# The second layer's root product and the output product of a graph network, in seven block products instead of whole ones

## The chip, the cores and the metric

The kernel runs on one core of a Trainium2 chip, as one launch. The metric is the device time of that launch in microseconds (us), lower is better; the times below are medians of several runs. A profile is one execution taken by the hardware profiler. Its span goes from the first to the last instruction, and the device time of the same execution is a little longer.

## The reference, cut to what matters

Two graph blocks follow each other on 384 nodes with 1024 features, each with a layer norm ahead of it and a residual around it. The first is an attention block over a mask of edges. The second is a relational graph convolution of two layers on 768 features. All is in float32.

```python
x = relu(h_text @ w_in + b_in)
for l in range(2):
    h_in = x
    # per relation r: mean over the edges of type r, of x @ W[r], W = comp x basis
    x = _rgcn_conv(x, src, dst, edge_type, basis[l], comp[l], root[l], conv_bias[l])
    #   = agg + x @ root[l] + conv_bias[l]
    x = relu(x) + h_in
    x = _batchnorm(x, bn_gamma[l], bn_beta[l])   # over the nodes
h_final = x @ w_out + b_out                       # 384 x 768 times 768 x 1024
out = x_before + _layernorm(h_final, ln_gamma, ln_beta)
```

Two products are touched: `x @ root[l]` of the second layer (384 x 768 times 768 x 768) and `x @ w_out`.

## The kernel before, in words

The queues of TensorE (PE), VectorE (DVE), GpSimd (POOL) and SyncE (SP) follow the order in which the code is written, and from line 496 on ScalarE (ACT) does too. So the place of a call in the code is its place in its engine's queue. Tiles come from pools, with the waits between engines put in by the framework: who overwrites a buffer waits for all its readers. PSUM has eight banks, dealt in turn by `next_bank`. Weights go through `wload`, which takes one of five buffers in turn; SP issues those loads in order, so a load whose buffer isn't free holds up the ones behind it.

Features lie on partitions in the convolution (`XT`, `XN`: six chunks of 128 features by 384 nodes). Many products in this kernel are already done by halves: the three operands are cut in two each way, and seven products of quarter size stand in for eight, with sums and differences of the quarters made by DVE beforehand and the partial results gathered behind. In code this is `multiply` (L399) for the attention part and the input layer (L402 in the profile), and the local `times` in the convolution (L979 for the products by basis, L1077 for the aggregation over nodes). The products that are not cut are one plain accumulation over the six chunks.

The second block runs so:

- The input layer (L857 to L903) writes `XT`. DVE and ACT gather its quarters (L882, L883).
- For each layer and each of four basis matrices b, `XT` times the basis (L985 and L979) gives `H_`. `weight_sums` and `last_sums` (L927 to L935) make the differences of the weights, `node_sums` (L920) those of the nodes. `go_between` puts other work between the products: in the second layer it is `mix`, by which the adjacency tables `A` of the six relations are weighted into `At` (L346 and L348).
- The root product (L1014 to L1023) accumulates all six output chunks in six banks, 36 matmuls of 384 columns (L1019). `rest()`, the last product of the basis before it, comes in behind the first six.
- The aggregation (L1080 to L1162) works on three pairs of output chunks. It first makes the differences of `At` (L1082 to L1086) and the first `feature_sums` (L1097). A product of each pair is added to the root's banks; `begin` (L1063) then moves the banks to `XN` on ACT, with the convolution's bias. All later products are added to `XN` by DVE in `take` (L1107). PE writes a bank again only when `take` has read it. When a chunk is complete, ACT applies the ReLU (`rectify`, L1110), DVE adds the residual and takes statistics (`measure`, L1042 to L1049), and `normalise_layer` (L1054 to L1058) ends the chunk.
- In the second layer the rows `b_out`, `ln_gamma` and `ln_beta` are loaded by ACT's queue into the room of `A` (L1038).
- The output (L1169 to L1198) goes by blocks of 128 nodes, t = 0, 1, 2. POOL first adds `ln_beta` to the residual `x_sb` (L1170). Per block, PE does six matmuls for each part of the 1024 columns (L1183); DVE adds `b_out` and takes statistics (L1187, L1189), ACT takes a square root (L159), and DVE makes the norm and the residual in two steps for each half (L1194, L1197). Each half is stored at once, one by SP, one by ACT.

Of the kernel before, what the change touches and what calls it, by code (L numbers as in the profile page):

```python
# [10 lines left out]
F32 = mybir.dt.float32  # L11
# [3 lines left out]
AF = mybir.ActivationFunctionType  # L15
ALU = mybir.AluOpType

P = 128
# [10 lines left out]
HC = DC // 2  # L29
HN = N // 2  # L30
# [21 lines left out]
def gnn_kernel(ctx: ExitStack, tc: tile.TileContext, out, x, edges, chunks, cols, rows, small,  # L52
               wq, wk, wv, wiq, wik, wiv, wo, w_in, basis, root, w_out):
# [299 lines left out]
    def add_up(r):  # L353
        sums[r] = late.tile([P, N], F32, tag="sum", name="sum", bufs=4)
        nc.gpsimd.tensor_tensor(sums[r], A[:, r, 0, :], A[:, r, 1, :], ALU.add)
        nc.gpsimd.tensor_tensor(sums[r], sums[r], A[:, r, 2, :], ALU.add)

    def share(r):

        ps = next_bank("ps_cnt", [i for i in range(8) if i not in taken])  # L360
        nc.tensor.matmul(ps[:, :N], ones, sums[r], start=True, stop=True)
        rn = late.tile([P, N], F32, tag="rn", name="rn", bufs=2)

        nc.scalar.activation(rn, ps[:, :N], AF.Relu, bias=minus)
        nc.scalar.activation(rn, rn, AF.Identity, bias=ones[:, 0:1])
        nc.vector.reciprocal(rn, rn)
        nc.vector.tensor_tensor(A[:, r], A[:, r], rn[:, None, :].to_broadcast([P, NT, N]), ALU.mult)
        if r + 4 < R:
            add_up(r + 4)


    with ExitStack() as inner:
# [263 lines left out]
        A = late.tile([P, R, NT, N], F32, tag="A", name="A")  # L636

# [93 lines left out]
        for g in range(STEPS + 1):  # L731
            f = g + LEAD
            if g < STEPS:
                turn_probs(g)
            if f < STEPS:
                exponents(f)
            if f - 1 in total:
                normalise(f - 1)
            if f + 1 < STEPS:
                scores(f + 1)  # L740
            if g == STEPS:
                ps_y = next_bank("ps_y", (0,))
                multiply_o(ps_y, 2, 0, range(KD - 1))
            if g > 0:
                gather(g - 1)
            if f + 2 == STEPS:

                w_x = [act_tile("w_x") for _ in range(2)]
                for half in range(2):
                    load_rows(w_x[half], w_in[half])  # L750
                w_first = [wload(basis[0, 0, part], (2, DC), "w_c") for part in range(3)]
                w_first += [wload(basis[0, 1, part], (2, DC), "w_c") for part in range(2)]
        soft_stack.close()
# [118 lines left out]
        for p in range(3):  # L872
# [13 lines left out]
            add_up_quad(quads[0][0], pb)  # L886
            multiply(pc, s[:, 0], T[1], True)
# [18 lines left out]
    with tc.tile_pool(name="conv", bufs=1) as cp:  # L906
# [7 lines left out]

        def node_sums(X):
            S = cp.tile([P, 4, 3, P], F32, tag="S", name="S")
            for i, a, b, op in ((0, block(X, 1, 0), block(X, 1, 1), ALU.add), (1, S[:, 0], block(X, 0, 0), ALU.subtract),
                                (2, block(X, 0, 0), block(X, 1, 0), ALU.subtract),
                                (3, block(X, 0, 1), S[:, 1], ALU.subtract)):
                nc.vector.tensor_tensor(S[:, i], a, b, op)  # L920
            return S

        def weight_sums(w):
            T13 = keep.tile([P, 3, 2, HC], F32, tag="hT", name="T13")
            T2 = keep.tile([P, 3, HC], F32, tag="mask8", name="T2")
            for c in range(3):
                nc.vector.tensor_tensor(T13[:, c], w[c][:, :, HC:], w[c][:, 0, :].rearrange("p (o d) -> p o d", o=2),  # L927
                                        ALU.subtract)
                nc.vector.tensor_tensor(T2[:, c], w[c][:, 1, HC:], T13[:, c, 0], ALU.subtract)
            return T13[:, :, 0], T2, T13[:, :, 1]  # L930

        def last_sums(w, T2):
            T4 = cp.tile([P, 3, HC], F32, tag="T4", name="T4")
            for c in range(3):
                nc.vector.tensor_tensor(T4[:, c], w[c][:, 1, :HC], T2[:, c], ALU.subtract)  # L935
            return T4
# [19 lines left out]
        for i in range(10):  # L956
            between[1, (i + 1) // 3, (i + 1) % 3] = mixes(1, 1 + i // 2, *((0, 1), (2, 3))[i % 2])

# [6 lines left out]
        for l in range(L):  # L965
# [3 lines left out]
            for b in range(B):  # L969
# [23 lines left out]
                times(pc, S[:, 0], lambda c: T[0][:, c], True)  # L993
# [3 lines left out]
                times(pa, S[:, 1], lambda c: T[1][:, c])  # L997
                nc.scalar.copy(hs[0][1], pa)
                times(pc, S[:, 3], lambda c: w[c][:, 1, HC:])
                nc.vector.tensor_tensor(hs[0][1], hs[0][1], pc, ALU.add)  # L1000
                times(pa, S[:, 2], lambda c: T[2][:, c])
# [12 lines left out]
            w = [wload(root[l, part], (2, DC), "w_c") for part in range(3)]  # L1014
            XN = xtp.tile([P, KC, N], F32, tag="XT", name="XN")
            pr = [next_bank("ps_c", [i for i in range(8) if i not in kept])[:, :N] for _ in range(KC)]
            for k in range(KC):
# [6 lines left out]
            room2 = keep.tile([P, KD * N], F32, tag="hT", name="room2")  # L1024
            spaces = [room2[:, 2304:]]
            if l + 1 < L:
                spaces += [v.rearrange("p i k o -> p (i k o)")[:, i * 768:(i + 1) * 768] for v, n in
                           ((cp.tile([P, 4, 3, P], F32, tag="S", name="sums"), 2),
                            (wpool.tile([P, 2, 6, P], F32, tag="w", name="sums"), 2)) for i in range(n)]
                spaces.append(cp.tile([P, 3, HC], F32, tag="T4", name="sums").rearrange("p c d -> p (c d)")[:, :768])  # L1030
                w = load_basis(l + 1, 0)
            else:

                room = late.tile([P, R * NT * N], F32, tag="A", name="room")
                spaces += [room[:, 3 * D + i * 768:3 * D + (i + 1) * 768] for i in range(5)]
                rowsB = room[:, :3 * D].rearrange("p (j d) -> p j d", j=3)
                for j, r in enumerate((R_BOUT, R_LNG, R_LNB)):
                    nc.scalar.dma_start(rowsB[:, j, :], rows[r:r + 1, :].to_broadcast([P, D]))  # L1038

# [31 lines left out]
            def q(i, j):  # L1071

                return At.rearrange("p b n d -> p (b n) d")[:, i * 6:i * 6 + 6, j * HN:(j + 1) * HN]

# [5 lines left out]
            T1, T2 = [room2[:, i * 1152:(i + 1) * 1152].rearrange("p (c d) -> p c d", c=6) for i in range(2)]  # L1080
            T4 = keep.tile([P, 6, HN], F32, tag="mask8", name="T4")
            nc.vector.tensor_tensor(T1, q(0, 1), q(0, 0), ALU.subtract)  # L1082
            nc.vector.tensor_tensor(T2, q(1, 1), T1, ALU.subtract)
            T3 = q(0, 1)
            nc.vector.tensor_tensor(T3, q(1, 1), q(0, 1), ALU.subtract)
            nc.vector.tensor_tensor(T4, q(1, 0), T2, ALU.subtract)  # L1086
# [32 lines left out]
            for p in range(pairs):  # L1119
                times(pr[2 * p][:, :HN], h(2 * p, 1), q(1, 0))  # L1120
            for o in range(KC):
                begin(o)
            take(0, 0, pa)
            ready = None
            for p in range(pairs):
# [11 lines left out]
                next(sums, None)  # L1137
                times(pc, S[p][3], q(1, 1))
# [23 lines left out]
                pa = following  # L1162
            XT = XN
# [5 lines left out]
        for t in range(NT):  # L1169
            nc.gpsimd.tensor_tensor(x_sb[:, t, :], x_sb[:, t, :], rowsB[:, 2, :], ALU.add)  # L1170
        w = [wload(w_out[part], (2, D), "w_out") for part in range(3)]
        hf_ = cp.tile([P, NT, D], F32, tag="H", name="hf")
        for t in range(NT):
            hf = hf_[:, t, :]
            last = t == NT - 1
            ps = [next_bank("ps_f") for _ in range(3 if last else 2)]

            parts = [(ps[0], 0, 512), (ps[1][:, :256], 512, 768), (ps[2][:, :256], 768, D)] if last else \
                [(ps[0], 0, 512), (ps[1], 512, D)]
            for ks in ((range(4), range(4, KC)) if t == 0 else (range(KC),)):  # L1180
                for p, c0, c1 in parts:
                    for k in ks:
                        nc.tensor.matmul(p, XT[:, k, t * P:(t + 1) * P], w[k // 2][:, k % 2, c0:c1],  # L1183
                                         start=(k == 0), stop=(k == KC - 1))
            st = tiny.tile([P, 4, 6], F32, tag="st", name="st")
            for p, c0, c1 in parts:
                nc.vector.tensor_tensor(hf[:, c0:c1], p, rowsB[:, 0, c0:c1], ALU.add)  # L1187
                for c in range(c0, c1, 256):
                    nc.vector.bn_stats(st[:, c // 256, :], hf[:, c:c + 256])  # L1189
            mv, sd = row_spread(st)  # L1190

            parts = ((nc.sync, slice(0, 512)), (nc.scalar, slice(512, D)))
            for _, cs in parts:
                nc.vector.scalar_tensor_tensor(hf[:, cs], hf[:, cs], mv[:, 0:1], rowsB[:, 1, cs], ALU.subtract, ALU.mult)  # L1194
            nc.vector.reciprocal(sd, sd)
            for queue, cs in parts:
                nc.vector.scalar_tensor_tensor(hf[:, cs], hf[:, cs], sd, x_sb[:, t, cs], ALU.mult, ALU.add)  # L1197
                queue.dma_start(out[t * P:(t + 1) * P, cs], hf[:, cs])  # L1198

# [70 lines left out]
```

## Time and profile before

| | us |
|---|---|
| device time, median of 3 runs (715.83 to 717.43) | 715.99 |
| the profiled execution: device time | 717.47 |
| the profiled execution: span | 715.7 |
| PE busy in the span | 699.9 |
| DVE busy in the span | 512.6 |
| ACT busy in the span | 157.6 |
| POOL busy in the span | 308.1 |
| second layer's root product, chain (L1019) | 611.18 to 636.34, with 1.94 of L979 in it |
| second layer's aggregation, chain (L1077) | 636.34 to 677.29 |
| output product, chain (L1183) | 677.29 to 708.23 |

How to read the views. The page gives each engine's busy time, and the span in 40 slices with the busy share of each in tenths; `PEclk` is the clock that TensorE was granted. A f32 matmul shows as two records, so 36 matmuls are x72. The chain of waits is followed back from the last instruction to whatever released each one, and printed in order of time: start, length, engine, what, line. The timeline gives the instructions of an engine: start, busy time, engine, line, operation, output and inputs, count; in brackets the idle time before it and what ended it. Matmuls overlap in the pipeline, so that a group's busy time is a little longer than its step.

### The profile page before, as it was taken

To read this page: it belongs to the slowest core of one execution; us is meant where nothing else is said; L and a number is where in the kernel's file an instruction comes from. 1 tells how busy PE (TensorE), PEld (TensorE's weight loads), DVE (VectorE), ACT (ScalarE), POOL (GpSimd) and SP (SyncE) were. 2 spreads that over 40 slices of the span, in tenths; PEclk is the share of its full clock that TensorE was granted. 3 is DMA by queue.
4 is the path that set the end of the run, shared out by engine and by line. 5 is a ranking of instruction groups with operands and counts; after the bars stand their busy time and mean duration, and the time that the engine had idled before them with its cause. 6 is when DMAs were issued, how large, how long until landed. Compare 5 with 4: busy or idle time off the path is not lost.

```text
span 715.7 us, 9149 instructions
## 1 busy us (share of the span) xinstructions
PE 699.9 (98%) x3228; PEld 527.9 (74%) x3228; DVE 512.6 (72%) x1307; ACT 157.6 (22%) x360; POOL 308.1 (43%) x239
## 2 busy tenths in 40 slices
PE   8999999999999999999999999999999999999995
PEld 7759999999997444478985555558975555579943
DVE  5886697868886699787534279798878766507756
ACT  3211111111111577410221124202131111011100
POOL 1366777778687788687786542000000000120000
PEclk9999999999999999999999999999999999999999
DMA  8788787373562622733424994311104322700001
GB/s 303 267 279 264 228 250 212 80 243 67 203 209 43 177 2 1 221 44 45 89 0 103 250 288 153 133 44 45 45 0 133 102 69 94 308 1 1 1 30 59
DMA packets 69180, 91.04 MB, mean 127 GB/s; under 512 B 22940, under 2 KB 50688, under 8 KB 68750
## 3 DMA queue, kind: packets, MB, share of 16 engines
q1 hardware_dynamic: 46830, 78.45, 32.6%
q0 software_dynamic: 21296, 9.60, 10.8%
q10 hardware_dynamic: 1008, 2.41, 0.9%
q8 instruction: 25, 0.41, 0.2%
q14 instruction: 21, 0.17, 0.1%
HBM read 79.27 MB, written 11.16 MB: 126 GB/s over the span
## 4 chain that ended last, share of the span: by engine, by line
PE 87%; DVE 10%; ACT 2%; DMA 1%; issue 0%; DVEq 0%; ACTq 0%
PE ps_g L985 12%; PE ps_g L979 10%; PE ps_k L402 10%; PE ps_c L1077 10%; PE ps_v L402 8%; PE ps_q L420 6%; PE ps_q L402 5%; PE ps_f L1183 4%; DVE At L348 4%; PE ps_y L402 3%; PE ps_c L1019 3%; PE ps_x L402 3%; PE ps_o L707 2%; PE ps_s L662 2%; PE ps_pT L696 2%; PE ps_v L586 2%
## 5 line engine op out<-in xcount | busy, mean ns | idle before, releaser
L283 POOL DMA_INDIRECT atab<-count,at x99 | 166.3, 1679 | 44.2 <-issue 23.5
L278 POOL DMA_INDIRECT mtab<-m_val,at x99 | 103.4, 1045 | 57.6 <-issue 22.9
L1170 POOL TENSOR_TENSOR x_sb<-x_sb,room 128x1024 f32<-128x1024 f32 x3 | 7.0, 2348 | 188.9 <-DMA room<-in_rows 188.9
L348 DVE SCALAR_TENSOR_TENSOR At<-A,small_sb,At 128x1152 f32<-128x1152 f32 x40 | 53.6, 1414 | 0.0
L979 PE MATMUL ps_g<-T,S 128*128 128x384 f32 x144 | 49.1, 486 | 0.0
L985 PE MATMUL ps_g<-w_c,XN 128*128 128x384 f32 x144 | 47.7, 487 | 1.1 <-DVE XN L1107 1.1
L985 PE MATMUL ps_g<-w_c,XT 128*128 128x384 f32 x144 | 47.9, 486 | 0.0
L420 PE MATMUL ps_q<-hT,w_q 128*128 128x384 f32 (+1 forms) x160 | 43.4, 435 | 1.4 <-DVE hT L108 1.4
L985 PEld LDWEIGHTS ps_g<-w_c,XN 128*128 128x128 f32 x144 | 27.3, 190 | 20.2 <-DVE XN L1107 1.4
L979 PEld LDWEIGHTS ps_g<-T,S 128*128 128x128 f32 x144 | 27.3, 190 | 19.2 <-ACT H L991 0.4
L985 PEld LDWEIGHTS ps_g<-w_c,XT 128*128 128x128 f32 x144 | 27.3, 190 | 18.8
L420 PEld LDWEIGHTS ps_q<-hT,w_q 128*128 128x128 f32 x160 | 30.1, 200 | 14.1 <-ACT hT L101 1.7
L1077 PE MATMUL ps_c<-At,H 128*128 128x192 f32 x216 | 36.4, 326 | 0.0
L1077 PEld LDWEIGHTS ps_c<-At,H 128*128 128x128 f32 x216 | 35.4, 190 | 0.5
L402 PE MATMUL ps_k<-T,S 128*128 128x192 f32 x192 | 35.1, 326 | 0.0
L1107 DVE TENSOR_TENSOR XN<-XN,ps_c 128x192 f32<-128x192 f32 x38 | 12.5, 349 | 30.8 <-ACT XN L1063 19.7
L402 PEld LDWEIGHTS ps_k<-T,S 128*128 128x128 f32 x192 | 31.8, 190 | 0.0
L1183 PE MATMUL ps_f<-w_out,XN 128*128 128x512 f32 (+1 forms) x84 | 31.1, 531 | 0.0
L675 DVE CUSTOM_DVE_ANT_0 s<-ps_s,mask 128x384 f32<-128x384 f32 x48 | 24.5, 550 | 5.3 <-PE ps_s L662 5.3
L267 DVE SCALAR_TENSOR_TENSOR same<-cells,own,later 128x128 f32<-128x128 int32 x99 | 28.0, 350 | 0.4
L267 DVE SCALAR_TENSOR_TENSOR same<-keys,key,weigh 128x128 f32<-128x128 int32 x99 | 27.9, 349 | 0.0
L1183 PEld LDWEIGHTS ps_f<-w_out,XN 128*128 128x128 f32 x84 | 15.9, 190 | 14.9 <-issue 14.3
(298 smaller groups left out, 1411.6 us busy)
## 6 DMA issues: line engine op xcount, KB each, us to landing
w_c<-in_basis SPq DMA_DIRECT2D x96, 192.0 KB, 4.1
atab<-zero SPq DMA_DIRECT2D x36, 192.0 KB, 5.2
A<-atab POOLq DMA_DIRECT2D x12, 576.0 KB, 9.0
keys<-keys_d SPq DMA_DIRECT2D x25, 192.0 KB, 5.1
w_c<-in_root SPq DMA_DIRECT2D x6, 768.0 KB, 7.1
w_q<-in_wiq SPq DMA_DIRECT2D x16, 256.0 KB, 6.4
w_k<-in_wk SPq DMA_DIRECT2D x16, 256.0 KB, 5.8
w_k<-in_wik SPq DMA_DIRECT2D x16, 256.0 KB, 3.0
```

Source lines behind the costliest of these rows:

```text
L267: nc.vector.scalar_tensor_tensor(same, row[:, n, :], mine[:, c:c + 1], times, ALU.is_equal, ALU.mult, accum_out=count[:, i, c:c + 1])
L278: nc.gpsimd.indirect_dma_start(mtab[c // PER][:, :], bass.IndirectOffsetOnAxis(at[:, 0, c:c + 1], 0), m_val[:, c:c + 1], None)
L283: nc.gpsimd.indirect_dma_start(atab[0 if i < 11 else i % 2][:, :], bass.IndirectOffsetOnAxis(at[:, 1, c:c + 1], 0), count[:, 1, c:c + 1], ...
L348: nc.vector.scalar_tensor_tensor(At[:, b], A[:, r], w, At[:, b], ALU.mult, ALU.add)
L402: nc.tensor.matmul(ps, a[:, k, :], b[:, k, :], start=start and k == 0, stop=(k == 3), skip_group_check=not start)
L420: nc.tensor.matmul(ps[o][:, c], wt_[:, k, o * P:(o + 1) * P], src[:, k, c], start=(k == 0 and c.start == 0), stop=(k == KD - 1 and c.stop ...
L675: nc.vector.tensor_tensor_reduce(s[j], ps[:, :N], mask8[:, t, :], -scale, 3.0e38, ALU.add, ALU.min, tops[:, j:j + 1])
L979: nc.tensor.matmul(ps, x[:, c], y(c), start=start and c == 0, stop=(c == 2), skip_group_check=not start)
L985: nc.tensor.matmul(ps, block(XT, n, i)[:, c], w[c][:, i, o * HC:(o + 1) * HC], start=(first and c == 0), stop=(c == 2 and (i == 1 or ps is ...
L1019: nc.tensor.matmul(pr[o], w[k // 2][:, k % 2, o * P:(o + 1) * P], XT[:, k, :], start=(k == 0), stop=(k == KC - 1))
L1077: nc.tensor.matmul(ps, x[:, c], y[:, c], start=start and c == 0, stop=stop and c == 5, skip_group_check=True)
L1183: nc.tensor.matmul(p, XT[:, k, t * P:(t + 1) * P], w[k // 2][:, k % 2, c0:c1], start=(k == 0), stop=(k == KC - 1))
```

## The change

It does four things.

1. The second layer's root product is cut like the others (`second_root`). The weights come in three thirds of 256 output columns (`root_thirds`, another layout of the second layer's matrix, four loads for each third). Each third takes seven products of three matmuls of 192 columns. `begin_root`, hung into the last basis of the second layer, loads the first two thirds, makes the differences of `XT` (`root_T`) and the sums of the first third's weights; the others follow inside the product. ACT and DVE gather the quarters straight into `XN`, so `begin` is left out there, and three products of the aggregation get banks of their own and a `take` each. The differences of `At` (`share_sums`) move into the second and third of the root's thirds.
2. The output product of node blocks 0 and 1 is cut in seven: two blocks of nodes, two halves of columns, `XT`'s odd and even chunks. `out_sums` makes the differences of `w_out` (`out_T`, twelve operations of 512 elements): four ahead of the aggregation, one at two places in each of the first two pairs, four in the last. The sums of the nodes (`OS`) come after the last chunk. `put_out` adds products to the output tile one by one. Block 2 stays whole; two of its matmuls come first and the other 16 last.
3. `finish` normalises block 0, and half of block 1, by an ACT step of scale and offset and two POOL steps (times `ln_gamma`, plus residual), stored by SP. The other half of block 1 and block 2 stay on DVE.
4. `ln_beta` is loaded into the tile `boB` by SP while the attention ends, and DVE adds it to `x_sb` in the input layer, in place of POOL's three additions at the output. Single tiles (`x_all`, `room2`, `mroom`, `sum_room`) replace several that were taken from the pools one at a time.

```diff
+            for t in {1: (0,), 2: (1, 2)}.get(p, ()):
+                nc.vector.tensor_tensor(x_sb[:, t, :], x_sb[:, t, :], boB, ALU.add)
             multiply(pc, s[:, 0], T[1], True)
...
+        def begin_root(c):
+            if c == 1:
+                between_mixes()
+                for t in range(2):
+                    root_w.append(wload(root_thirds[t], (KC, HC2), "w_c"))
...
+                for i, x, y in ((0, x_quarter(0, 1), x_quarter(0, 0)), (1, x_quarter(1, 1), root_T[0]),
+                                (2, x_quarter(1, 1), x_quarter(0, 1)), (3, x_quarter(1, 0), root_T[1])):
+                    nc.vector.tensor_tensor(root_T[i], x, y, ALU.subtract)
+            else:
+                rooms.append(late.tile([P, R * NT * N], F32, tag="A", name="room"))
+                root_S.append(root_sums(0))
...
+        def second_root(rest):
+            root_w.append(wload(root_thirds[2], (KC, HC2), "w_c"))
...
+            for p in range(3):
+                s, T = root_S[p], root_T
+                pa, pb, pc = [next_bank("ps_c", range(8))[:, :HN] for _ in range(3)]
...
+                times(pa, root_block(p, 0, 0), x_quarter(0, 0), True)
+                nc.scalar.activation(quads[0][0], pa, AF.Identity, bias=bs[0])
+                rest()
+                times(pb, root_block(p, 0, 1), x_quarter(1, 0), True)
+                nc.vector.tensor_tensor(quads[0][0], quads[0][0], pb, ALU.add)
+                times(pc, s[:, 0], T[0], True)
+                nc.scalar.activation(quads[1][1], pc, AF.Identity, bias=bs[1])
+                if p < 2:
+                    root_S.append(root_sums(p + 1))
+                times(pa, s[:, 1], T[1])
+                nc.scalar.activation(quads[0][1], pa, AF.Identity, bias=bs[0])
+                times(pc, s[:, 3], x_quarter(1, 1))
+                nc.vector.tensor_tensor(quads[0][1], quads[0][1], pc, ALU.add)
+                if p:
+                    next(shares_)
+                times(pa, s[:, 2], T[2])
+                nc.vector.tensor_tensor(quads[1][1], quads[1][1], pa, ALU.add)
+                if p:
+                    next(shares_)
+
+                def rest(pa=pa, x=root_block(p, 1, 1), quad=quads[1][0], b=bs[1]):
+                    times(pa, x, root_T[3])
+                    nc.scalar.activation(quad, pa, AF.Identity, bias=b)
...
+                w_end = [wload(w_out[part], (2, D), "w_out") for part in range(3)]
...
+                out_sums((0, 0), (1, 0), (0, 1), (1, 1))
...
                 times(pa, S[p][1], T2)
                 take(o0, 1, pa)
                 next(sums, None)
+                if l + 1 == L:
+                    out_sums(*(((0, 2), (1, 2), (2, 2), (3, 2)) if last else ((2, p),)))
                 times(pc, S[p][3], q(1, 1))
...
                 ready = measure(rectify(o1))
                 pa = following
+                if l + 1 == L:
+                    out_sums((3, p))
...
+        third(*parts[0], 0, 1)
+        pa, pb, pc, pd = [next_bank("ps_f") for _ in range(4)]
+        times(pa, block(XT, 0, 0), b_end(0, 0), True)
+        put_out(0, 0, pa, True, False)
+        times(pb, block(XT, 0, 1), b_end(1, 0), True)
+        put_out(0, 0, pb, False, True)
+        times(pc, OS[0], summed(0), True)
+        put_out(1, 512, pc, True, False)
+        times(pa, OS[1], summed(1))
+        put_out(0, 512, pa, True, False)
+        times(pc, OS[3], b_end(1, 1))
+        put_out(0, 512, pc, False, True)
+        times(pd, block(XT, 1, 1), summed(3), True)
+        put_out(1, 0, pd, True, False)
+        times(pa, OS[2], summed(2))
+        finish(0)
+        put_out(1, 0, pa, False, True)
+        put_out(1, 512, pa, False, True)
+        third(*parts[0], *range(2, KC))
+        for p, c0 in parts[1:]:
+            third(p, c0, *range(KC))
+        finish(1)
+        for p, c0 in parts:
+            put_out(2, c0, p, True, True)
+        finish(2)
```

## The prediction

> **What bounds the kernel now.** I read the page's busy times and slices first, then the chain of waits from 585 us on, then the timeline of VectorE (DVE) and TensorE (PE) over the last 110 us, which is all that the change touches except for one row load.
>
> ```profile
> span 715.7 us, 9149 instructions
> PE 699.9 (98%) x3228; PEld 527.9 (74%) x3228; DVE 512.6 (72%) x1307; ACT 157.6 (22%) x360; POOL 308.1 (43%) x239
> PE   8999999999999999999999999999999999999995
> DVE  5886697868886699787534279798878766507756
> PEclk9999999999999999999999999999999999999999
> ```
>
> PE is busy in every slice at full granted clock, so PE work that goes away can shorten the span. DVE's last four slices (7756) say that it isn't idle there. The chain says what ends last:
>
> ```profile
> 611.18 3.87 PE ps_c L1019 x12
> 615.05 1.94 PE ps_g L979 x6
> 616.99 19.35 PE ps_c L1019 x60
> 636.34 40.95 PE ps_c L1077 x252
> 677.29 30.94 PE ps_f L1183 x84
> 708.26 0.43 DVE hf L1187
> ```
>
> From the second root product (L1019) to the last output matmul (L1183) there is not one wait. Each f32 matmul is two records. A microsecond of PE removed here is a microsecond of span, unless DVE, which feeds PE, falls behind. How much room it has is seen in the aggregation loop (L1077, L1107), first DVE, then PE:
>
> ```profile
> 660.76 0.35 DVE L1107 TENSOR_TENSOR XN<-XN,ps_c 128x192 f32<-128x192 f32 x1
> 661.02 0.95 DVE L1097 TENSOR_TENSOR room<-room,H 128x768 f32<-128x768 f32 x1
> 661.89 0.35 DVE L1107 TENSOR_TENSOR XN<-XN,ps_c 128x192 f32<-128x192 f32 x1
> 664.37 0.34 DVE L1107 TENSOR_TENSOR XN<-XN,ps_c 128x192 f32<-128x192 f32 x1
> ```
>
> ```profile
> 661.52 4.07 PE L1077 MATMUL ps_c<-At,H 128*128 128x192 f32 x24
> 665.42 2.11 PE L1077 MATMUL ps_c<-T,H 128*128 128x192 f32 x12
> ```
>
> PE may add into a bank again only when DVE has read it. The add of 660.76 ends at 661.11 and the products that need it start at 661.52: 0.41 us of room. The add of 664.37 ends at 664.71, its products start at 665.42: 0.71. The others, read alike, have 0.8 to 1.1. This is the narrow place.
>
> **PE: what goes.** Root: 72 records took 3.87 + 19.35 = 23.22 us. In its place stand 3 thirds x 7 products x 3 matmuls = 63 matmuls, 126 records of 192 columns. L1077 is the row of that shape: 40.95 / 252 = 0.1625 us, so 20.48. Gain 2.74. Output: 84 records (60 of 512 columns, 24 of 256) are 36,864 columns in 30.94 us, 0.839 ns each. After it: 7 x 3 matmuls of 512 columns for two node blocks, and the third block as before, 33,792 columns, 28.36 us. Gain 2.58. Together 5.32 us.
>
> **DVE and the queues up to the loop.** I number by the old times.
> - The last norm's bias row is now added to x by DVE in the input layer: 3 adds at 1.22 (row L540). One follows the add at 355.80, before a wait of 2.44 for PE; two follow 362.48, before a wait of 4.85. Hidden. Its 0.5 MB load goes on SP's queue behind five weight loads; the next load behind it waits for a buffer in any case, and from 358 to 376 us the DMA moves 0 GB/s. Cost zero, at worst the microsecond of one late add.
> - Four node differences (576 elements, between 0.56 for 384 and 0.95 for 768: 0.75 each) and four weight sums (384) are 5.1 us after the mixes end at 602.5. Before, DVE then waited 6.34 us for PE until 609.36. Hidden; the first two thirds of the root weights take the buffers and the times (588.57) of the old root loads.
> - Inside the root product DVE gets 2 x 2.1 us of weight sums, 9 adds of 0.35 and the four share differences (1.35 each, before at 611.7), 12.8 us beside 22.4 of PE. ScalarE (ACT) empties each bank in 0.40 while PE does another product of 0.97: about 0.3 to spare. One order hurts: in the second third a share difference stands ahead of the add that frees the bank of the next carried-over product. I get PE 0.19 late, and 0.10 for a restart (192-column groups of 8 records step by 1.40 instead of 1.30 after a wait, at 350.09): 0.29.
> - Four output-weight differences (512 elements: 0.61 apart, 0.72 where one needs the one before, the steps of L396) are 2.7 us, and the first feature sums 3.6, done about 641.4 of the new clock. PE has 8.8 us of products that need neither, until 641.5. Hidden, and L1063's ACT work is gone. SP loads the third third and two w_out parts as buffers come free near 609; the last w_out part waits for the first third's buffer, free near 621, and is wanted at 670. On ACT's queue the two row loads wait behind the root's evacuations; only the last root evacuation is behind them, wanted 45 us later.
>
> **DVE in the loop.** This I stepped through instruction by instruction with the trace's durations and both engines in order; for the kernel before, the same stepping gives PE's end at 677.30 (trace 677.29) and the last normalised chunk at 682.2 (trace 682.05). Pairs 0 and 1 get two differences of 0.61 each. The first fills a wait of 0.73. The other three push the adds: PE is late by 0.14 at the place with 0.41 us of room, by 0.24 at the place with 0.71, by 0.39 at the first add of the last pair; with three restarts 1.07 us. The last pair gets four (2.55 us) ahead of the add that starts its normalisation. The last chunk is then ready 6.5 us after the first output matmul instead of 4.8; PE has seven matmuls that don't need it, 7 x 0.86 = 6.02. Late 0.53, with the restart 0.63. The four sums after it are ready one by one with 0.4 us and more to spare.
>
> **The end.** PE's last 18 matmuls (10.3 us) belong to the third block, as before. Behind the last product of the first two blocks DVE has two adds with statistics (2.8), the finish of block one (2.7) and the third block's first 768 columns (2.2). It is free 0.7 us before PE ends, so the tail (708.26 to 715.7) moves as it is. POOL has no row of 512 elements: 0.99 us for 384 and 2.35 for 1024 give 1.26. Six of them, from 696.3 on in the new clock, end at 703.9; their three stores on SP are issued before the last block's, which is queued behind them at 707. One row of 384 took 1.53 (409.03) beside a DVE add; at that ratio the six end at 708, just when the last block's stores come up, so even this bound costs next to nothing. ACT's three steps before them have no row either; 1024 elements took 1.24 in L452, so 0.65 each, on an engine that does nothing else there. Its three adds of x (L1170) go, from where it was alone.
>
> Here a rule speaks against the change. The rows:
>
> ```profile
> 434.37 1.00 POOL L356 TENSOR_TENSOR sum<-sum,A 128x384 f32<-128x384 f32 x1
> 434.79 0.56 DVE L1002 TENSOR_TENSOR H<-H,ps_g 128x384 f32<-128x384 f32 x1 [0.43 <-PE ps_g L979]
> 435.26 0.95 DVE L927 TENSOR_TENSOR T<-w_c 128x768 f32<-128x768 f32 x1
> ```
>
> DVE's L927 has two SBUF inputs and starts 0.11 us before POOL ends, in its usual step. The Trainium skill ("SBUF — State Buffer", "Who interferes with whom") says that a DVE instruction with two SBUF inputs and a GpSimd instruction that reads SBUF exclude each other, the later one waiting for the whole of the other. Block one's finish has two such DVE instructions while POOL works. By the rows they cost nothing; by the rule up to 2 x 1.26 us, less the 0.7 to spare: 1.8. An overlap of 0.11 is little evidence, so the rule stays in the range; I take the rows.
>
> **Sum.** -5.32 + 0.29 + 1.07 + 0.63 = -3.33 us. The profiled execution took 717.47 (span 715.7, and 1.8 around it), 1.5 above the median of 715.99; the difference is carried over: 715.99 - 3.3 = 712.7.
>
> **Rivals.**
> 1. DVE hides everything: 715.99 - 5.3 = 710.7. For it: DVE is busy only 24.3 of the 36.3 us of the loop. Against: the free time isn't where the adds are. 0.13.
> 2. POOL's lock decides the end: gain 1.5, 714.5. It would show as two long DVE instructions in block one's finish. 0.16.
> 3. DVE becomes the bound from the loop on: none of the eight differences (5.0) and four sums (2.1) is hidden, 7.1 against 5.3, so +1.8, 717.8. It decides once more than 5.3 us reach PE. For it: each late add moves PE one for one, and the first rooms are 0.4 and 0.7. Against: the later rooms and the one wait of 0.73 take part of it, and PE's own delay makes room for the next add. 0.10.
> 4. The root doesn't get cheaper because its records are ruled by weight loads (PEld 190 ns each, 126 x 0.19 = 23.9): gain 2.6 - 0.7 - 2.0, nothing left, 716. L1077 has the same loads and steps by 0.1625. 0.03.
>
> **How the numbers follow.** My forecast, 711.6 to 713.7, has 0.58. A measurement of this kernel tells 0.3% (2.15 us) from no change, so faster means under 713.84: my case, rival 1 and a quarter of rival 2 (the lock in part), 0.75. Same: the rest of rival 2, and rival 4, 0.15. Slower: rival 3, 0.10. The range runs from rival 1's edge, 710.9, to 715.2, past rival 2; rivals 3 and 4 and the last of rival 1 are left out.
>
> **What would show it.** Right: the root near 20.5 us and the output near 28.4 of PE by the chain; three waits of PE on DVE's adds in the loop of 0.1 to 0.4 us and one of about 0.5 on the last chunk; POOL near 1.26 us each, the same tail. Wrong: waits of PE in the loop that add up to over 2 us, a chain that ends through POOL and SP (POOL over 2.7 us an operation would do that and cost the whole gain), or any new wait before 611 us.

## The result and the profile after

The changed kernel takes 713.15 us (median of 6 runs, 712.45 to 714.33) against 716.00 for the kernel before on the same chip (6 runs, 715.83 to 717.60). The ratio is 0.9954 [0.9943, 0.9965]: faster by some 3.3 us, more than the 0.3% that such a measurement can tell, near the 712.7 forecast and inside its range.

The runs of most kernels here fall on two levels, some 1.3 to 3.5 us apart, so that a median of six can lie on either. I therefore compare kernels by one stage of their profiled executions: from the root product's first matmul row to DVE's first addition to the last piece of the last output block (704.91 in the chain below). It took 97.24 us before and takes 93.66 now, 3.58 less. A second profiled execution of the changed kernel, on another chip, has 93.67. The span fell by only 3.1 (715.7 to 712.6): the stage starts 0.23 later, a shift that stands already at 332 us, in the attention part, before the first instruction that the edits change; and from 704.91 on the tail is 0.25 longer, in the landing of the last store, not in DVE (3.56 us there, 3.62 before).

From the page of the changed kernel, its busy times and two of its rows of slices:

```profile
span 712.6 us, 9327 instructions
PE 696.3 (98%) x3276; PEld 534.1 (75%) x3276; DVE 541.0 (76%) x1354; ACT 161.5 (23%) x369; POOL 315.0 (44%) x242
PE   8999999999999999999999999999999999999995
...
PEclk9999999999999999999999999999999999999999
```

PE has 48 records more, yet is busy 3.6 us less: the root's 126 records have 192 columns where its 72 had 384, and the output has 6 records fewer, of 512 columns. DVE is busy 28.4 us more. The clock is the same. What DVE's new work cost is told by the chain of waits, where before there was nothing but PE from the root to the last block:

```profile
614.32 10.74 PE ps_c L1024 x66
...
625.16 0.35 DVE XN L1045
625.51 1.27 DVE room L983
626.78 0.28 DVE XN L1049
...
627.10 6.12 PE ps_c L1024 x36
...
682.26 14.00 PE ps_f L1332 x32
696.26 8.63 PE ps_f L1343 x32
...
704.91 0.43 DVE hf L1301
```

(L1024 is the root's `times`, L983 the share differences, L1045 and L1049 the root's adds, L1332 the output's seven products, L1343 its whole block.) The first wait is the one foretold in the root: the share difference of 1.27 stands ahead of the add at 626.78 that frees the bank, and PE goes on at 627.10. Between 653.7 and 682.26 the chain runs through DVE, where the aggregation waits. PE's own timeline has the four places (the brackets give idle time and what ended it; an idle time too short to be marked shows in the start times alone):

```profile
659.45 4.17 PE L1188 MATMUL ps_c<-At,H 128*128 128x192 f32 x24
663.59 2.22 PE L1188 MATMUL ps_c<-mroom,H 128*128 128x192 f32 x12
...
669.88 2.22 PE L1188 MATMUL ps_c<-At,room 128*128 128x192 f32 x12 [0.17 <-DVE XN L1215]
...
682.26 1.12 PE L1332 MATMUL ps_f<-w_out,XN 128*128 128x512 f32 x2 [0.26 <-DVE XN L1173]
```

24 records step by 3.90 and 12 by 1.95, so behind the group at 667.60 the next is due at 669.55; it starts at 669.88, 0.33 late. In the same way 659.45 is 0.07 late and 663.59 is 0.14 late, and each restart (the first group after a wait) steps 0.10 longer than usual (4.17 and 2.22 where undisturbed groups have 4.06 and 2.11). The aggregation takes 34.00 us from its first seven-product row to the first output row; before, it took 33.14. On DVE's timeline, L1148 is a difference of output weights and L1215 the `take` that PE waits for:

```profile
668.88 0.68 DVE L1148 TENSOR_TENSOR sum_room<-w_out,x_all 128x512 f32<-128x512 f32 x1
669.48 0.35 DVE L1215 TENSOR_TENSOR XN<-XN,ps_c 128x192 f32<-128x192 f32 x1
...
671.18 0.68 DVE L1148 TENSOR_TENSOR x_all<-w_out 128x512 f32<-128x512 f32 x1
...
673.11 0.68 DVE L1148 TENSOR_TENSOR sum_room<-w_out,x_all 128x512 f32<-128x512 f32 x1
673.71 0.35 DVE L1215 TENSOR_TENSOR XN<-XN,ps_c 128x192 f32<-128x192 f32 x1
```

The difference at 668.88 pushes the add to 669.48; it ends at 669.83 and PE starts 0.05 later. The four from 671.18 on hold the add at 673.71, which the last chunk waits for, and that chunk is ready 0.4 us after PE runs out of other products at 681.84 (it goes on at 682.26, 0.42 late).

The end is where GpSimd and DVE meet. The timeline of both, with the finish of block 1 (DVE L1322 and L1326) and GpSimd's last three steps (L1318, L1319):

```profile
700.20 0.74 DVE L1322 SCALAR_TENSOR_TENSOR hf<-hf,mv,room 128x512 f32<-128x512 f32 x1
...
700.34 1.73 POOL L1319 TENSOR_TENSOR hf<-hf,x_sb 128x512 f32<-128x512 f32 x1
700.98 1.64 DVE L1326 SCALAR_TENSOR_TENSOR hf<-hf,sd,x_sb 128x512 f32<-128x512 f32 x1
702.03 1.72 POOL L1318 TENSOR_TENSOR hf<-hf,room 128x512 f32<-128x512 f32 x1
702.54 0.68 DVE L1301 TENSOR_TENSOR hf<-ps_f,room 128x512 f32<-128x512 f32 x1
...
703.83 1.27 POOL L1319 TENSOR_TENSOR hf<-hf,x_sb 128x512 f32<-128x512 f32 x1
```

DVE's L1326 takes 1.64 where the same instruction takes 0.75 when GpSimd is idle, and GpSimd's two take 1.73 and 1.72 where its others take 1.27. No time was lost by it: DVE is free at 704.80, PE's last matmul ends at 704.88.

### The profile page after: what moved, and what is told of

Same layout as the page of the kernel before. It is cut to its first block, busy times and chain, and to the rows that moved or that the text cites. A ratio compares the mean times of both kernels' runs of the same rounds, so it can differ in the third digit from the quotient of the medians.

```text
span 712.6 us, 9327 instructions
## 1 busy us (share of the span) xinstructions
PE 696.3 (98%) x3276; PEld 534.1 (75%) x3276; DVE 541.0 (76%) x1354; ACT 161.5 (23%) x369; POOL 315.0 (44%) x242
## 4 chain that ended last, share of the span: by engine, by line
PE 82%; DVE 14%; ACT 2%; issue 1%; DMA 1%; DVEq 0%; ACTq 0%
PE ps_g L1085 13%; PE ps_g L1079 10%; PE ps_k L403 10%; PE ps_v L403 9%; PE ps_c L1188 7%; PE ps_q L421 6%; PE ps_q L403 5%; DVE At L349 4%; PE ps_y L403 3%; PE ps_x L403 3%; PE ps_c L1024 3%; PE ps_o L709 2%; PE ps_v L587 2%; PE ps_f L1332 2%; PE ps_s L664 2%; PE ps_pT L698 2%
## 5 line engine op out<-in xcount | busy, mean ns | idle before, releaser
L279 POOL DMA_INDIRECT mtab<-m_val,at x99 | 105.1, 1062 | 56.3 <-issue 24.1
L1318 POOL TENSOR_TENSOR hf<-hf,room 128x512 f32<-128x512 f32 x3 | 4.3, 1421 | 257.7 <-ACT hf L1316 257.7
L1079 PE MATMUL ps_g<-room,x_all 128*128 128x384 f32 x96 | 33.6, 486 | 0.0
L1079 PEld LDWEIGHTS ps_g<-room,x_all 128*128 128x128 f32 x96 | 18.3, 190 | 12.7
L1100 DVE TENSOR_TENSOR H<-H,ps_g 128x384 f32<-128x384 f32 x8 | 4.4, 554 | 27.5 <-PE ps_g L1079 27.5
L938 DVE TENSOR_TENSOR room<-w_c 128x768 f32<-128x768 f32 x24 | 24.8, 1032 | 0.0
L1122 PE MATMUL ps_c<-XT,w_c 128*128 128x384 f32 x72 | 23.5, 486 | 0.0
```

What stands on the lines that cost most here:

```text
L279: nc.gpsimd.indirect_dma_start(mtab[c // PER][:, :], bass.IndirectOffsetOnAxis(at[:, 0, c:c + 1], 0), m_val[:, c:c + 1], None)
L1079: nc.tensor.matmul(ps, x[:, c], y(c), start=start and c == 0, stop=(c == 2), skip_group_check=not start)
L1122: nc.tensor.matmul(pr[o], w[k // 2][:, k % 2, o * P:(o + 1) * P], XT[:, k, :], start=(k == 0), stop=(k == KC - 1))
```

## The experiments

Theory: the change gains the matmul columns that it removes (5.32 us by the prediction's count) and pays back what DVE's additions reach PE late, at the places where DVE had little room. Against it stand the rivals: that the seven-product records don't get cheaper with their columns, that the waits come from the root's part and not from where the output-weight differences stand, that GpSimd's finish decides the end, and that DVE is simply too busy. The first four kernels ran on a chip where all kernels scattered more (the kernel before: 727.60, 720.39 to 746.48), so that their ratios have wide intervals and the stage carries the reading. The other four ran on a quiet one (before: 716.04, 715.89 to 717.61).

**The root alone in seven products; the output product as before.**

```diff
-                out_sums((0, 0), (1, 0), (0, 1), (1, 1))
...
-                if l + 1 == L:
-                    out_sums(*(((0, 2), (1, 2), (2, 2), (3, 2)) if last else ((2, p),)))
...
-        OS = [mroom.rearrange("p c n -> p (c n)")[:, i * N:(i + 1) * N] for i in range(3)] + [room2[:, :N]]
...
+        for t in range(NT):
             hf = hf_[:, t, :]
...
+            last = t == NT - 1
...
```

> Only the second root is cut; the output product is whole and ends as in the kernel before, and the loop gets no differences of w_out. My theory (PE columns minus the waits of PE on late DVE adds): root -2.74 + 0.27 for the one late add in the root, no waits in the loop, none at the output: 716.0 - 2.5 = 713.5 us, PE in the root 20.5 us by the chain, aggregation 40.95 less the three products' own banks, output 30.9 us as before. Rival A (the whole gain comes from the output and its new end, the root only shifts work to DVE): 715.5 or more, with waits of PE in the root of 2 us.

Measured: 726.21, ratio 0.9962 [0.9933, 0.9991]; the stage took 94.86, 2.38 less than before. PE's timeline:

```profile
632.23 1.24 PE L1024 MATMUL ps_c<-sum_room,w_c 128*128 128x192 f32 x6
...
646.95 2.11 PE L1187 MATMUL ps_c<-room 128*128 128x192 f32 x12
...
680.10 31.09 PE L1294 MATMUL ps_f<-w_out,XN 128*128 128x512 f32 x84
```

The group at 632.23 is the root's one wait: the row ahead of it starts at 630.99 and would let it start at 631.96. From 646.95 to 680.10 the aggregation takes 33.15, as before the change, with no wait, though the `At` differences and the three separate `take`s have moved. So the root's part brings its columns (2.74 by the prediction's count) less 0.36, of which 0.27 is the wait and 0.10 the restart, and adds nothing to the loop's length.

**The output alone in seven products; the root whole.**

```diff
-            if l:
-                rest = second_root(rest)
-            else:
-                w = [wload(root[part], (2, DC), "w_c") for part in range(3)]
...
+            w = [wload(root[l, part], (2, DC), "w_c") for part in range(3)]
...
-            if l == 0:
-                for _ in share_sums():
-                    pass
+            for _ in share_sums():
+                pass
+            if l:
+                out_sums((0, 0), (1, 0), (0, 1), (1, 1))
```

> Only the output is cut, the second root is whole as in the kernel before; the differences of w_out stand where the change has them, the first four ahead of the first feature sums. My theory: output -2.58, waits in the loop 0.87 and on the last chunk 0.54 as in the changed kernel: 716.0 - 1.2 = 714.8 us. If the waits come from the root's new work leaving DVE late at the loop's start (rival B), they are gone here: 716.0 - 2.6 = 713.4 us.

Measured: 728.01, ratio 0.9993 [0.9963, 1.0022], which can't tell it from the kernel before; the stage took 96.34, 0.90 less. PE's timeline has the waits at the same places as in the changed kernel:

```profile
671.88 4.17 PE L1181 MATMUL ps_c<-At,H 128*128 128x192 f32 x24
676.09 2.22 PE L1181 MATMUL ps_c<-mroom,H 128*128 128x192 f32 x12
...
682.44 2.22 PE L1181 MATMUL ps_c<-At,room 128*128 128x192 f32 x12 [0.23 <-DVE XN L1209]
...
694.93 1.12 PE L1319 MATMUL ps_f<-w_out,XN 128*128 128x512 f32 x2 [0.37 <-DVE XN L1166]
```

The aggregation takes 34.19 (1.05 over), the output 29.20 where 28.56 is what it takes undisturbed (shown further down). The waits are there without the root's part, so they belong to the output-weight differences, and the rival that puts them on the root falls. The two parts alone make 2.38 + 0.90 = 3.28, together 3.58. The 0.30 lies in the aggregation and the output, which wait 0.19 and 0.12 longer here. DVE isn't late when this loop starts: it waits 17.60 us ahead of the `take` at 651.12, and 4.95 for PE ahead of the next, at 656.42. What differs is when ScalarE's ReLU (`rectify`) is done, for which DVE's `measure` waits. In this kernel:

```profile
674.22 0.56 DVE L1150 TENSOR_TENSOR XN<-XN 128x384 f32<-128x384 f32 x1 [0.65 <-ACT XN L1212]
```

The same place in the changed kernel:

```profile
661.72 0.56 DVE L1157 TENSOR_TENSOR XN<-XN 128x384 f32<-128x384 f32 x1 [0.59 <-ACT XN L1218]
```

In all six chunks DVE waits 0.06 to 0.07 longer here, as it does in the kernel before. PE's four waits start late by 0.13, 0.21, 0.39 and 0.53 here, by 0.07, 0.14, 0.33 and 0.42 in the changed kernel: 0.06 or 0.07 for one ReLU ahead of each of the first three, 0.11 for two ahead of the last. Every kernel here with the root cut has the shorter wait; why the ReLU comes sooner there stays open.

**The differences on GpSimd, all issued ahead of the aggregation.** The last three results lie in the tile from which the root's last carried-over product still reads its nodes' differences, so this kernel overwrites one operand of that product before it is read.

```diff
-                        nc.vector.tensor_tensor(out_T[i][:, c], x(c), y(c), ALU.subtract)
+                        nc.gpsimd.tensor_tensor(out_T[i][:, c], x(c), y(c), ALU.subtract)
...
-                out_sums((0, 0), (1, 0), (0, 1), (1, 1))
+                out_sums(*[(i, c) for c in range(3) for i in (0, 1)], *[(i, c) for c in range(3) for i in (2, 3)])
```

(The `out_sums` of the loop are gone.)

> All twelve differences of w_out on GpSimd, issued ahead of the loop; the rest is the changed kernel. My theory: PE's waits in the loop (0.87) and most of that on the last chunk (0.54) go, since DVE is as free in the loop as it was before: 713.15 - 1.4 = 711.7 us. GpSimd takes 1.27 us each and ends near 644. Rival C (the shared port decides): GpSimd's fifteen microseconds hold DVE's instructions with two SBUF inputs, up to 0.9 us each as seen once in block one's finish, and DVE is 3 to 5 us late at the loop's start: 713 us or more, with DVE's differences of At and feature sums over 1.5 us each.

Measured: 734.16, ratio 1.0076 [1.0047, 1.0105], slower. It doesn't answer what it was made for: that carried-over product is ordered with GpSimd's writes, and PE waited for GpSimd 4.25 us at 650.70 and 2.33 at 654.57. Two readings stand all the same. The aggregation and the last chunk have no wait, and DVE's instructions with two SBUF inputs grow beside GpSimd: the feature sums to about 2.0 from 0.95, two of the `At` differences to 2.16 and 2.15 from 1.35.

**The finish of blocks 0 and 1 on DVE again.**

```diff
-            aside = parts[:NT - 1 - t]
+            aside = ()
```

> All three blocks are finished by DVE, as in the kernel before; the rest is the changed kernel. My theory: finish of block 0 takes DVE 2.3 us more, of which 0.9 fits into its wait for PE, and block 1 takes 0.9 more but is rid of the 0.89 us that one instruction was held; the last block's last part starts 0.5 to 0.7 us later: 713.15 + 0.6 = 713.75 us. Rival D (the finish aside is what makes the new order possible): DVE is late by the whole 3.2 us, 716 us. Rival C (GpSimd's port costs more than the finish aside brings): 713.15 or less.

Measured: 727.85, ratio 0.9994 [0.9965, 1.0024]; the stage took 94.64, 0.98 more than with the finish aside. Its chain at the end, with PE's last row of work (L1343) gone from it:

```profile
695.89 11.44 PE ps_f L1332 x26
707.35 0.69 DVE hf L1301
...
715.93 1.42 DVE hf L1326 x2
...
719.52 0.33 DVE hf L1301
```

From 707.35 on the chain is DVE's own, to the end: PE's last matmul ends at 718.50 by its timeline, 1.0 us before DVE comes to the last piece. So the finish on ScalarE and GpSimd is worth 1.0 us, more than the 0.5 to 0.7 that I expected, and far from all of the 4.1 us of steps that it takes off DVE (three halves of 0.66 and 0.71 by these rows).

**Each late difference made twice** (the eight issued in the loop; the four ahead of it once).

```diff
-                        nc.vector.tensor_tensor(out_T[i][:, c], x(c), y(c), ALU.subtract)
+                        for _ in range(1 if (i, c) in ((0, 0), (1, 0), (0, 1), (1, 1)) else 2):
+                            nc.vector.tensor_tensor(out_T[i][:, c], x(c), y(c), ALU.subtract)
```

> Each of the eight differences of w_out inside the loop is issued twice in a row (the second writes the same values); the rest is the changed kernel. From the root's first matmul to the last part's first add of block 2 the changed kernel takes 93.66 us (the kernel before 97.24). My theory (a late add moves PE one for one, once the room is used): the stepping with the trace's durations gives 4.6 us more, 98.2 us, and device time of 1.0 us over the kernel before. Rival E (DVE's lateness is mostly absorbed in its waits; PE's waits of 0.9 us in the loop are a fixed cost of the restarts): 1 us more or less, 94.7 us.

Measured: 718.75 (718.02 to 719.93), ratio 1.0032 [1.0020, 1.0045], slower than the kernel before; the stage took 99.09, 5.43 over the changed kernel. PE's timeline:

```profile
658.30 2.22 PE L1189 MATMUL ps_c<-At,room 128*128 128x192 f32 x12 [0.62 <-DVE XN L1216]
660.61 4.17 PE L1189 MATMUL ps_c<-At,H 128*128 128x192 f32 x24
665.48 2.22 PE L1189 MATMUL ps_c<-mroom,H 128*128 128x192 f32 x12 [0.70 <-DVE XN L1216]
...
672.49 2.22 PE L1189 MATMUL ps_c<-At,room 128*128 128x192 f32 x12 [0.90 <-DVE XN L1216]
...
683.30 2.84 PE L1333 MATMUL ps_f<-w_out,XN 128*128 128x512 f32 x6 [1.26 <-DVE XN L1174]
687.78 1.12 PE L1333 MATMUL ps_f<-w_out,XN 128*128 128x512 f32 x2 [1.63 <-DVE XN L1174]
```

The same places, longer, and new ones beside them. It missed my 4.6 in size: a pair of differences from 656.58 lets the next add start at 657.90, 1.32 later, where one alone takes 0.60, so the repeat costs 0.72 and not 0.61. Eight of 0.72 are 5.8, of which 5.43 reached PE. So the first set of differences has used up the room in the loop; what comes on top goes to the end nearly in full.

**The same differences, placed in DVE's waits.** Nothing is added or left out. The two `At` differences of the root's second third come behind its adds. The output weights are loaded inside the root, five of their differences are made in its third third, four more and the rest of the `At` differences behind the root, two between the carried-over `take`s, and one in the first pair.

```diff
+                else:
+                    out_sums((0, 0), (1, 0), (0, 1), (1, 1))
...
-                if p:
-                    next(shares_)
+                if p == 2:
+                    out_sums((0, 2))
...
-                if p:
+                if p == 1:
+                    next(shares_)
                     next(shares_)
...
+            if l:
+                out_sums((1, 2), (2, 0), (2, 1), (2, 2))
+                for _ in later_shares[0]:
+                    pass
...
+                if p < 2:
+                    out_sums((3, p))
...
-                    out_sums(*(((0, 2), (1, 2), (2, 2), (3, 2)) if last else ((2, p),)))
+                if l + 1 == L and p == 0:
+                    out_sums((3, 2))
```

> All twelve differences of w_out and all four of At stay on DVE, but stand in waits of DVE inside the root product and ahead of the loop (one in the first pair, where DVE has a wait of 0.73). My theory: the late add in the root (0.27), those in the loop (0.86) and most of the wait on the last chunk (0.54) go, 93.66 - 1.6 = 92.0 us for the stage, 711.5 us against 716.0, the best of all so far. Rival E: the stage stays within 0.3 us of 93.66. Rival F: the work only moves the lateness to the loop's start; PE waits for S0, S1 or the first takes there, 93 to 94 us.

Measured: 711.01 (710.81 to 714.37), ratio 0.9923 [0.9910, 0.9936]; the stage took 91.92. Its chain, whole from the root to the last block:

```profile
612.82 0.97 PE ps_c L1041 x6
613.79 1.94 PE ps_g L1102 x6
615.73 18.52 PE ps_c L1041 x114
634.25 1.95 PE ps_c L1195 x12
636.20 0.97 PE ps_c L1041 x6
637.18 39.00 PE ps_c L1195 x240
676.18 1.72 PE ps_f L1354 x4
677.89 18.02 PE ps_f L1343 x42
695.92 8.63 PE ps_f L1354 x32
```

PE again from end to end, no wait left. The stage is 97.24 - 91.92 = 5.32 us shorter than before the change: to the hundredth the columns that the prediction counted. DVE is busy as long as in the changed kernel (541.3 against 541.0), so it was never too busy; its work stood in the wrong place. This version beats both kernels.

**The differences on GpSimd again, the last three behind the root's last carried-over product.**

```diff
+                out_sums(*[(i, c) for c in range(3) for i in (0, 1)], *[(2, c) for c in range(3)])
...
                 rest()
+                out_sums(*[(3, c) for c in range(3)])
```

> All twelve differences of w_out on GpSimd; the last three, which overwrite an operand of the root's last carried-over product, now stand behind it. After the first try DVE instructions with two SBUF inputs took about 2.0 us instead of 0.95 beside GpSimd. By that: two differences of At and four feature sums are held by 0.8 to 1.05 us each, 5.8 in all, less the 2.7 that DVE no longer does there: S0 and the first adds about 3 us late, PE waits 1.5 to 3 us ahead of the loop, which itself has no waits (-0.86) and none on the last chunk (-0.54): stage 94 to 95.5 us. If port sharing didn't matter: 92.3 us.

Measured: 712.24 (711.43 to 713.47), ratio 0.9941 [0.9927, 0.9955]; the stage took 92.28, so my 94 to 95.5 was wrong. The timeline, first DVE, then GpSimd:

```profile
632.48 2.16 DVE L983 TENSOR_TENSOR mroom<-At,room 128x1152 f32<-128x1152 f32 x1
634.56 2.02 DVE L1205 TENSOR_TENSOR room<-H 128x768 f32<-128x768 f32 x1
...
640.39 0.95 DVE L1205 TENSOR_TENSOR room<-H,room 128x768 f32<-128x768 f32 x1
```

```profile
633.38 6.27 POOL L1148 TENSOR_TENSOR sum_room<-w_out,x_all 128x512 f32<-128x512 f32 x3
```

The holding is real: while GpSimd works, until 639.65, DVE's sums take twice their time, and the first one after it takes 0.95 again; GpSimd's three take 6.27 instead of 3 x 1.27. But it falls where PE has 8.8 us of products that need none of it. Only the root's wait is left (at 625.42, late by 0.26, and its restart), and the stage is the placed version's 91.92 and that 0.36. I had the size of each holding right, about 1 us for a feature sum and 0.8 for an `At` difference, and forgot the cover.

**The changed kernel beside the last three**: 714.13 (712.75 to 714.29), ratio 0.9959 [0.9945, 0.9973], stage 93.67: the reading of the first profile repeats on the second chip.

> The changed kernel itself, on the chip of these three runs: 0.995 of the kernel before; stage 93.66 us within 0.1.

## Why the prediction was right

*PE's columns, -5.32.* Right. The placed version shows it bare, 5.32. That a record of 192 columns costs 0.1625 although its weight load takes 0.19 held in the root too; the rival that denied it falls with the root-only kernel.

*The root's wait, +0.29.* Right in place and cause, a little too small: 0.27 late where I had 0.19, at the share difference ahead of the add, and 0.10 for the restart, together 0.36 by the root's length (30.58 us from its first row to the loop's 641.83, against 30.22 in the placed version).

*The loop, +1.07.* Right in its three places, a little too large: 0.86. Late by 0.07, 0.14 and 0.33 where I had 0.14, 0.24 and 0.39; the three restarts of 0.10 came as foretold. I had stepped through the loop with the ReLU as the kernel before has it. The output-only kernel, whose ReLU comes as before, is late by 0.13, 0.21 and 0.39, and by 0.53 on the last chunk: within 0.03 of the forecast. So the steps were sized right, and what I didn't foresee is the ReLU that comes 0.06 sooner in the changed kernel.

*The last chunk, +0.63.* Right in place, a little too large, for the same reason: 0.52. The output took 29.08 against 28.56 in the placed version.

*The sum.* -5.32 + 0.36 + 0.86 + 0.52 = -3.58, the measured stage; I had -3.33. I had put everything outside the stage at nothing, the tail included, and there the profiled execution lost 0.23 ahead of it and 0.25 behind it. That its span, 3.1 shorter, lies so near to 3.33 is in part luck: the errors inside and outside the stage have opposite signs.

*What was costed at nothing.* The three x adds of 1.22 in the input layer are there, and behind them DVE still waits 1.30 and 2.57 us for PE. The node differences and first weight sums are done at 606.6, and DVE then waits 2.48 for PE. No new wait shows before 611 us. The last `w_out` part landed a little after 625, by the DMA's busy share, and was first read at 671.18.

*The end.* The step that failed here cost no time. I trusted the trace's rows over the rule of the Trainium skill ("SBUF — State Buffer", "Who interferes with whom"), and the rule was right: of block 1's two DVE instructions, one was held 0.89. The other, at 700.20, came 0.14 ahead of GpSimd, which had to wait in its place (1.73). So my upper bound, both held for the whole of GpSimd's 1.26, was too high. DVE is free 0.08 before PE ends, so without the holding it would have been 0.97, a little more than my 0.7, and that covered the 0.89. GpSimd ended at 705.1 instead of 703.9, again with time left before the last block's store at 708.50. ScalarE's steps were 0.76 to 0.81, not 0.65.

*Rivals.* That DVE hides everything was false for this order and true for another: the placed version is that rival's 5.3. That DVE becomes the bound was false; it would have needed more than 5.32 us of waits to reach PE, and 1.74 did (93.66 less 91.92). With the differences doubled 7.17 did, and the gain became a loss. GpSimd's lock was real and missed the path by 0.08 us.

## What to carry to other kernels

Where one engine runs without a wait, count the columns or bytes that an edit takes off it; then go through the engine that feeds it instruction by instruction, since only the room behind each instruction counts, not its idle total (24.3 us busy of 36.3 were no help to an add with 0.4). Side work whose inputs are ready early goes into the feeder's own waits or behind products that don't need it; here the same instructions in another order were worth 1.7 us more. Work moved to GpSimd beside DVE instructions with two SBUF inputs lengthens both, which is harmless only where a cover can be named.

## What the hardware showed that I had not expected

DVE's instructions with two SBUF inputs and GpSimd's take turns nearly instruction by instruction. After GpSimd's end at 702.07, DVE's L1326 still ran 0.55 of its 0.75; after DVE's ends at 700.94 and 702.62, GpSimd ran 1.13 of its 1.27 both times. So all but the first 0.14 to 0.20 us of an instruction waits for the other engine. DVE's add at 702.54, with one input in PSUM, took its usual 0.68 beside GpSimd. The short part that isn't held would also explain the row on which the prediction relied, where DVE started 0.11 before GpSimd's end and showed nothing: the overlap was shorter than that part. This is read off three rows, whose lengths come back to the hundredth at the end of the last kernel with the differences on GpSimd (1.73, 1.64 and 1.72); it was not tried by itself.
